# Edge sums of a graph network: from a TensorE product in step 0 to u8 rows, VectorE and ScalarE in step 1

## The chip, the cores and the metric

The kernel runs on one core of a Trainium2 chip. The metric is the device time of one execution in microseconds (us). A core has five engines with a queue each: TensorE (PE, with weight loads as PEld), VectorE (DVE), ScalarE (ACT), GpSimd (POOL) and SyncE (SP, which here only starts transfers). ScalarE and GpSimd start transfers from their queues too.

## The reference

Four graph layers over 4096 nodes with 256 features; `adj` is a 4096 x 4096 float32 matrix of zeros and ones. Each layer is followed by a residual and a layer norm.

```python
# layer 0: deg = adj.sum(1); relu([x, adj @ x / max(deg, 1)] @ W + b)
# layer 1: R = (adj + I) / row sum; two steps n = 0, 1:
#   A  = top-p attention of Xa: softmax(q k^T), keep the largest until their sum is 0.9
#   Xf = R @ Xf ; Xa = A @ Xa ; Z += Xf @ U1[n].T + Xa @ U2[n].T
# layer 2 (the change concerns its edge term):
neighbor_node_features = adj @ node_features
neighbor_edge_features = jnp.einsum('ij,ji->i', adj, edge_features)[:, None]   # edge_features = adj
support = jnp.concatenate((node_features, neighbor_node_features, neighbor_edge_features), axis=1)
out = support @ weight + bias
# layer 3: relu((d^-1/2 (adj + I) d^-1/2 @ x) @ W + b)
```

The edge term is one number per node: the sum over j of adj[i,j] * adj[j,i].

## The kernel before

Nodes go in 32 tiles of 128 (NT = 32). A row of 4096 columns is worked in NLC = 8 pieces of LC = 512 columns, which is GP = 4 blocks of 128. Layer 0 loads the adjacency blocks with transfers from GpSimd that cast float32 to u8, multiplies, and leaves a u8 copy in DRAM (`adj8_d`). Layers 1 to 3 read that copy with SP.

Layer 1 is `run_step(n)` for n = 0, 1. Its loop over i from -2 to 31 is pipelined: while tile i is applied, the logits of tile i+2 are made, and the selection of tile i+1 runs on VectorE. `pieces` walks the eight pieces g of an iteration. For each it emits: the logits of the next tile (L385, copied out by ScalarE at L386); in step 0 the sparse product with gathered rows (L734; gathers on GpSimd at L643), in step 1 four transposes (L717), their copy `at` on ScalarE (L720) and the product with `xa` (L742); then `neighbours`, one piece of an R product (adjacency loaded by SP at L652, cast by ScalarE at L654, multiplied at L657); then the operations that `run_step` has put at piece g. The latter hold the largest values (L404), exponentials (L423 in step 0, L427 in step 1), the search for the threshold, `settle` with passes over the row (L629, L634) and the layer norm, whose power is taken on GpSimd (L194). Rows whose threshold needs more care are put off and worked as jobs between the tiles; a conditional block on VectorE stands in each job.

In step 0 `neighbours` also makes the edge sums: `adjn`, the blocks of the other orientation, is loaded by GpSimd with a cast to u8 (L663), cast by ScalarE (L666), and multiplied with the same weights as R (L669) into the bank `nef_ps`. The diagonal of the 128 x 128 result is taken on VectorE at L683 and written to a column of `nef`. Layer 2 reads `nef` at L1110. Because `nef_ps` takes the bank "nef", R products of step 0 all use the bank "acc".

The order on each engine is fixed when the program is built: a scheduler takes the instructions in the order of the program text, lets ready ones pass those that wait, and works with estimated durations. `issue_after(x)` puts instructions on x's engine behind x. A pool's tile with `bufs=k` has k buffers, and a writer waits until the readers of k tiles ago are done.

Of the kernel before, what the change touches and what calls it, by code (L numbers as in the profile page):

```python
# [45 lines left out]


@with_exitstack
def gnn_stack(ctx, tc, x, adjt, adjn, w0, b0, w1, w2t, w3t, u1t, u2t, ln_g, ln_b, w2, b2, w3, b3, out):

# [59 lines left out]
    list_d = [dram.tile([N + P, 1], I32, name=f"list{n}_d") for n in range(STEPS)]  # L112

    adj8_d = [dram.tile([P, NT, P], U8, name=f"adj8_{it}_d") for it in range(NT)]
    h_d = dram.tile([N + P, D], F32, name="h_d")
    k_d = dram.tile([N + P, P], F32, name="k_d")

# [207 lines left out]

    with tc.tile_pool(name="l1", bufs=1, reuse_waits="tile") as l1:

        cur = {"late": False, "n": 0, "nef_done": False}


        FIRST = [[range(k * NT // 16, (k + 1) * NT // 16) for k in range(2)]]
# [313 lines left out]

        GP = LC // P

        def neighbours(n, i, g, acc_r, pn, xf):

            if g % 2 == 0:  # L650
                cur["a8"] = cur["w"].tile([P, 2 * GP, P], U8, tag="adj8", name="adj8", bufs=3)
                nc.sync.dma_start(cur["a8"], adj8_d[i][:, g * GP : (g + 2) * GP, :])  # L652
            a = cur["w"].tile([P, GP, P], F32R, tag="adjq", name="adjq", bufs=2)
            nc.scalar.copy(a, cur["a8"][:, g % 2 * GP : (g % 2 + 1) * GP, :])  # L654
            for j in range(GP):
                jt = g * GP + j
                nc.tensor.matmul(acc_r, a[:, j, :], xf[:, jt, :], start=(jt == 0), stop=False)  # L657
            if g + 1 == NLC:
                nc.tensor.matmul(acc_r, ident_r, xf[:, i, :], start=False, stop=True)
            if pn is not None:  # L660
                if g % (NLC // 2) == 0:
                    cur["b8"] = cur["w"].tile([P, NT // 2, P], U8, tag="adjn8", name="adjn8", bufs=2)
                    nc.gpsimd.dma_start(cur["b8"], adjn[i, :, g * GP : g * GP + NT // 2, :])  # L663
                b = cur["w"].tile([P, GP, P], F32R, tag="adjn", name="adjn", bufs=2)
                k = g % (NLC // 2) * GP
                nc.scalar.copy(b, cur["b8"][:, k : k + GP, :])  # L666
                for j in range(GP):
                    jt = g * GP + j
                    nc.tensor.matmul(pn[:, :P], a[:, j, :], b[:, j, :], start=(jt == 0),  # L669
                                     stop=(jt == NT - 1))  # L670

        def r_acc(i):

            return ps_acc.tile([P, 512], F32, tag=("acc", "nef")[i % 2 if cur["nef_done"] else 0], name="acc_r", bufs=1)

        def r_end(i, acc_r, pn):
            xf_new = work.tile([P, D], F32, tag="xf_new", name="xf_new", bufs=1)
            nc.scalar.activation(xf_new, acc_r[:, :D], AF.Copy, scale=rs[:, i : i + 1])
            nc.vector.scalar_tensor_tensor(xf_new, acc_r[:, D:], rs[:, i : i + 1], xf_new, op0=ALU.mult, op1=ALU.add)
            if pn is not None:  # L680

                junk = spare_row.bitcast(F32)[:, :P]
                nc.vector.scalar_tensor_tensor(junk, pn[:, :P], 1.0, ident, op0=ALU.mult, op1=ALU.mult,  # L683
                                               accum_out=nef[:, i : i + 1])
            nc.sync.dma_start(rows(xf_d, i), xf_new)

        def r_product(n, i, xf):

            acc_r, pn = r_acc(i), None
            if n == 0:  # L690
                pn = ps_acc.tile([P, 512], F32, tag="nef", name="nef_ps", bufs=1)
            for g in range(NLC):
                neighbours(n, i, g, acc_r, pn, xf)
            r_end(i, acc_r, pn)

        def pieces(n, st, nxt, ops, rs_now=()):


            G = GP
            few = st is not None and sparse(st)  # L700
            if st is not None:
                e = st["e"]
                acc_a = half("acc")
                if "xf" not in st:
                    fetch(n, st)
            with_r = st is not None and len(rs_now) > 0
            if with_r:
                i, = rs_now
                acc_r, pn = r_acc(i), None
                if n == 0:  # L710
                    pn = ps_acc.tile([P, 512], F32, tag="nef", name="nef_ps", bufs=1)
            ats = {}

            def turn(g):
                ps = ps_tr.tile([P, 4, P], F32, tag="tr", name="at_ps")
                for j in range(G):
                    nc.tensor.transpose(ps[:, j, :], e[:, (g * G + j) * P : (g * G + j + 1) * P], ident)  # L717
                at = cur["w"].tile([P, G, P], F32, tag="at", name="at", bufs=2)
                ats[g] = at
                nc.scalar.copy(at[:, :G, :], ps[:, :G, :])  # L720

            if st is not None and not few:
                turn(0)
            for g in range(NLC):
                if nxt is not None:
                    logits_chunk(nxt["e"], nxt["q"], g)
                if few:
                    per = KEPT // NLC
                    for k in range(g * per, (g + 1) * per):
                        if k % 4 == 0:  # L730
                            dg = cur["w"].tile([P, 4, P], F32, tag="at", name="dg", bufs=2)
                            nc.vector.tensor_mul(dg, ident[:, None, :].to_broadcast([P, 4, P]),
                                                 st["w"][:, k : k + 4, None].to_broadcast([P, 4, P]))
                        nc.tensor.matmul(acc_a, dg[:, k % 4, :], st["G"][k], start=(k == 0), stop=(k == KEPT - 1))  # L734
                        if k + 8 < KEPT:
                            gather(st, k + 8)
                elif st is not None:
                    if g + 1 < NLC:
                        turn(g + 1)
                    for j in range(G):  # L740
                        jt = g * G + j
                        nc.tensor.matmul(acc_a, ats[g][:, j, :], cur["xa"][:, jt, :], start=(jt == 0),  # L742
                                         stop=(jt == NT - 1))
                if with_r:
                    neighbours(n, i, g, acc_r, pn, cur["xf"])
                for f in ops.get(g, ()):
                    f()
            if st is None:
                for i in rs_now:
                    r_product(n, i, cur["xf"])  # L750
            else:
                xa_new = work.tile([P, D], F32, tag="xa_new", name="xa_new", bufs=1)
                nc.scalar.activation(xa_new, acc_a, AF.Copy, scale=st["sc"])
                if n + 1 < STEPS:
                    put(xa_d, st, xa_new)
                st["xa"] = xa_new
            if with_r:
                r_end(i, acc_r, pn)

        def put(dst, st, t):  # L760

# [27 lines left out]
        def mix(n, st):  # L789

            xt = transposed(st["xf"], st["xa"])
            ps = half("mm")
            for c in range(4):
                u = cur["u1" if c < 2 else "u2"]
                nc.tensor.matmul(ps, xt[:, c, :], u[:, c % 2, :], start=(c == 0), stop=(c == 3))  # L795
            h = work.tile([P, D], F32, tag="h", name="h")
            nc.vector.tensor_add(h, ps, st["res"])
            if n + 1 < STEPS:
                put(h_d, st, h)

                ps = half("mm")
                for c in range(2):
                    nc.tensor.matmul(ps[:, :P], xt[:, 2 + c, :], w3t_sb[:, c, :], start=(c == 0), stop=(c == 1))
                up = upper(ps[:, :P])
                kt = work.tile([P, P], F32, tag="kt", name="kt", bufs=1)
                nc.scalar.copy(kt[:, :DA], up[:, :DA])
                nc.vector.tensor_sub(kt[:, DA:], ps[:, DA:P], up[:, DA:])
                put(k_d, st, kt)
            return h
# [107 lines left out]
        def run_step(n, es):  # L917
# [37 lines left out]
            for i in range(-2, NT):  # L955
# [21 lines left out]
                if 0 < i + 2 < NT - 1:  # L977
                    turned = []
                    g = 1 if n else 6
                    at(g - 1, lambda i, turned: turned.append(transposed(cur["xa"][:, i + 3, :])), i, turned)  # L980
                    at(g, lambda turned: cur["qs"].append(query(None, turned[0])), turned)
                if cd is not None:
                    peak_groups(cd)
                    at(1, exp_rows, cd)
# [32 lines left out]
            if n == 0:  # L1017
# [4 lines left out]
                cur["late"] = True  # L1022
                fetch(n, jobs[0]["st"])
                cur["late"] = False
                cur["nef_done"] = True
                for i in range(FIRST[1][0][0]):
                    r_product(1, i, cur["next"])
            todo = []
            if n > 0:

                z_room(es[1 - NT % 2])
# [167 lines left out]
```

## Time and profile before

| | us |
|---|---|
| median of 3 runs (lowest to highest) | 3316.28 (3312.99 to 3319.80) |
| the profiled execution | 3319.24 |
| its span, first to last instruction | 3317.5 |

The mean granted TensorE clock is 0.967 of full speed. Busy shares of the span: TensorE 91%, VectorE 72%, ScalarE 57%, GpSimd 24%. These are means over stages that differ. The writes of `xa_new` (L753) mark the tiles: in step 0 from 476.5 to 1337.6, in step 1 from 1526.7 to about 2561; layers 2 and 3 fill the time from 2785 to the end. A row of the page's groups gives line, engine, operation, output and input tiles, count, then busy time, mean duration in ns, and the engine's idle time just before with what ended it.

### The profile page before, as it was taken

Reading aid. Unit: us, or ns where it says so; the run is one execution under the profiler, and the core shown is the slowest. Engines: PE = TensorE matmul, PEld = TensorE weight load, DVE = VectorE, ACT = ScalarE, POOL = GpSimd, SP = SyncE. Lnnn points to the kernel's source line nnn. Section 1 sums busy time; section 2 is a strip of 40 time slices with the busy share of each in tenths; the row PEclk is TensorE's granted clock in tenths of the full one; section 3 lists DMA queues with packets and bytes.
Section 4 is the critical chain, followed back from the end, with each engine's and each line's share of the span. In section 5 each row is a group of like instructions: output and inputs, shape, how many; then the busy total and the mean of one; then the engine's idle time right before and its main releaser. Section 6 shows DMA issues by size and latency. Waiting matters only on the chain. (4 is left out here: it accounts for less than half of the span.)

```text
span 3317.5 us, 46380 instructions
## 1 busy us (share of the span) xinstructions
PE 3005.6 (91%) x14600; PEld 2455.0 (74%) x14600; DVE 2392.3 (72%) x7113; ACT 1883.1 (57%) x3170; POOL 782.1 (24%) x916
## 2 busy tenths in 40 slices
PE   4999878999999997789989898989999786999998
PEld 4888767888888885567877777777788544888886
DVE  5888858878777776357988897888799673444444
ACT  4555566777777774455545454555455333666664
POOL 1111146666666665100000001000100001000000
PEclk9999989999999998889999999999999898999999
DMA  8888367777777776241000211011011133333332
GB/s 161 140 140 139 72 104 126 139 138 139 138 132 140 138 135 140 63 131 32 24 23 25 33 36 32 25 32 39 25 37 30 42 131 125 110 108 107 102 108 81
DMA packets 247906, 300.30 MB, mean 91 GB/s; under 512 B 34688, under 2 KB 201536, under 8 KB 247648
## 3 DMA queue, kind: packets, MB, share of 16 engines
q0 software_dynamic: 46624, 105.07, 22.7%
q1 hardware_dynamic: 184576, 176.73, 18.6%
q10 hardware_dynamic: 16448, 15.42, 1.5%
q8 instruction: 118, 1.93, 0.3%
q14 instruction: 140, 1.15, 0.1%
HBM read 331.17 MB, written 66.58 MB: 120 GB/s over the span
## 5 line engine op out<-in xcount | busy, mean ns | idle before, releaser
L657 PE MATMUL acc_r<-xh,adjq 128*128 128x512 f32 x2048 | 615.1, 431 | 25.3 <-ACT adjq L654 13.4
L742 PE MATMUL acc_bank<-xa,at 128*128 128x256 f32 x2304 | 569.6, 388 | 33.0 <-ACT at L720 32.5
L643 POOL DMA_INDIRECT G<-x_d,cols x512 | 499.4, 975 | 300.7 <-PE acc_bank L734 161.9
L742 PEld LDWEIGHTS acc_bank<-xa,at 128*128 128x128 f32 x2304 | 425.2, 194 | 94.8 <-ACT at L720 43.3
L654 ACT CAST adjq<-adj 128x512 fp32r<-128x512 uint8 x512 | 316.0, 619 | 294.5 <-PE acc_r L657 94.5
L657 PEld LDWEIGHTS acc_r<-xh,adjq 128*128 128x128 f32 x2048 | 380.4, 192 | 120.0 <-ACT adjq L654 43.5
L404 DVE MAX8 cand<-e 128x8 f32<-128x256 f32 x1024 | 381.9, 416 | 93.0 <-ACT e L386 92.0
L194 POOL TENSOR_TENSOR rstd<-ve,mhalf 128x1 f32<-128x1 f32 x168 | 102.3, 609 | 1374.4 <-DVE ve L192 1336.7
L386 ACT COPY e<-lg 128x512 f32<-128x512 f32 x552 | 319.0, 584 | 177.4 <-PE lg L385 176.4
L385 PE MATMUL lg<-kS,q 128*128 128x512 f32 x1104 | 393.5, 442 | 9.9 <-ACT e L386 9.6
L1093 ACT CAST a<-a 128x1024 fp32r<-128x1024 uint8 x256 | 268.0, 1048 | 147.5 <-PE acc L1096 119.3
L734 PE MATMUL acc_bank<-G,dg 128*128 128x256 f32 x1024 | 276.6, 390 | 51.5 <-DMA G<-x_d,cols 40.4
L501 DVE FIND_INDEX8 cols<-top,e 128x8 uint32<-128x4096 f32 x64 | 282.8, 4419 | 0.0
L1096 PE MATMUL acc<-xh,a 128*128 128x512 f32 x1024 | 254.9, 402 | 16.9 <-ACT a L1093 13.2
L170 PE MATMUL acc<-xh,a 128*128 128x512 f32 x1024 | 257.9, 404 | 13.3 <-ACT a L253 13.3
L734 PEld LDWEIGHTS acc_bank<-G,dg 128*128 128x128 f32 x1024 | 194.0, 193 | 101.1 <-DMA G<-x_d,cols 48.9
L720 ACT COPY at<-at_ps 128x512 f32<-128x512 f32 x296 | 173.6, 588 | 114.0 <-PE at_ps L717 90.1
L1096 PEld LDWEIGHTS acc<-xh,a 128*128 128x128 f32 x1024 | 190.5, 189 | 60.3 <-ACT a L1093 15.2
L1096 PE MATMUL acc<-yh,a 128*128 128x512 f32 x1024 | 233.7, 390 | 0.0
L170 PEld LDWEIGHTS acc<-xh,a 128*128 128x128 f32 x1024 | 191.7, 190 | 55.1 <-ACT a L253 13.5
L1096 PEld LDWEIGHTS acc<-yh,a 128*128 128x128 f32 x1024 | 192.1, 188 | 39.8
L253 ACT CAST a<-a 128x1024 fp32r<-128x1024 uint8 x128 | 133.9, 1048 | 129.6 <-PE acc L170 117.4
(282 smaller groups left out, 5001.5 us busy)
## 6 DMA issues: line engine op xcount, KB each, us to landing
adj<-adj_d SPq DMA_DIRECT2D x256, 128.0 KB, 2.7
a<-adj_d SPq DMA_DIRECT2D x256, 128.0 KB, 2.3
a<-in_adjt POOLq DMA_DIRECT2D x64, 256.0 KB
adj_d<-a SPq DMA_DIRECT2D x64, 256.0 KB, 3.7
adjn<-in_adjn POOLq DMA_DIRECT2D x64, 256.0 KB
x_d<-x SPq DMA_DIRECT2D x65, 128.0 KB, 1.8
G<-x_d,cols POOLq DMA_INDIRECT x512
xf_d<-xf_new SPq DMA_DIRECT2D x64, 128.0 KB, 4.9
```

Source lines behind the costliest of these rows:

```text
L170: nc.tensor.matmul(acc, a[:, j, :], halves(jt), start=(jt == 0), stop=(jt == NT - 1))
L385: nc.tensor.matmul(pl[:, :LC], q[k], kS[:, s], start=(k == 0), stop=(k == 1))
L386: nc.scalar.copy(l[:, s], pl[:, :LC])
L404: nc.vector.max(dst[:, 8 * g : 8 * g + 8], src[:, g * GW : (g + 1) * GW])
L501: nc.vector.max_index(st["at"][:, 8 * r : 8 * r + 8], t8, st["e"][:, :N])
L643: nc.gpsimd.indirect_dma_start(out=g, out_offset=None, in_=x1_d, in_offset=bass.IndirectOffsetOnAxis(ap=st["at"][:, k : k + 1], axis=0))
L654: nc.scalar.copy(a, cur["a8"][:, g % 2 * GP : (g % 2 + 1) * GP, :])
L657: nc.tensor.matmul(acc_r, a[:, j, :], xf[:, jt, :], start=(jt == 0), stop=False)
L734: nc.tensor.matmul(acc_a, dg[:, k % 4, :], st["G"][k], start=(k == 0), stop=(k == KEPT - 1))
L742: nc.tensor.matmul(acc_a, ats[g][:, j, :], cur["xa"][:, jt, :], start=(jt == 0), stop=(jt == NT - 1))
L1093: nc.scalar.copy(a, a8)
L1096: nc.tensor.matmul(acc, a[:, j, :], halves(jt), start=(jt == 0), stop=(jt == NT - 1))
```

## The change

The product of step 0 goes: `adjn` is no longer an input, and with it go L663, L666, L669 and L683. Instead `adj` and its transpose come in as plain rows (`adjr`, `adjc`). In step 1 each piece g of iteration i starts one transfer on GpSimd for tile i+2 (`edge_cast`), DRAM to DRAM, which casts 128 x 1024 float32 (512 KB) to u8 (128 KB): even g for `adjr`, odd g for `adjc`, eight per tile, 256 in all.

For the tile that is being applied, `edge_sums` runs once per piece in three stages. Two loads on ScalarE's queue bring 128 x 512 bytes of both (`r8`, `c8`, two buffers each). One piece later VectorE takes their bitwise AND, read as 128 x 128 int32, into `r8`. Another piece later ScalarE copies `r8` to `c8` with an accumulated sum into a column of `ns`; after the eighth piece VectorE adds the eight columns into `nef`. Loads and sums are put behind the latest `at` copy of ScalarE. What is left after the last tile is finished there.

Further: `adj8` is loaded per piece (64 KB, 512 loads) instead of per two pieces (128 KB, 256 loads), with three buffers as before; R products alternate between the banks "acc" and "nef" in step 0 too; `kt` moves to the pool of the step.

```diff
...
+    adjr8_d, adjc8_d = ([dram.tile([P, N], U8, name=f"{k}_{it}_d") for it in range(NT)] for k in ("adjr8", "adjc8"))
...
-        def neighbours(n, i, g, acc_r, pn, xf):
-
-            if g % 2 == 0:
-                cur["a8"] = cur["w"].tile([P, 2 * GP, P], U8, tag="adj8", name="adj8", bufs=3)
-                nc.sync.dma_start(cur["a8"], adj8_d[i][:, g * GP : (g + 2) * GP, :])
+        def neighbours(i, g, acc_r, xf):
+
+            a8 = cur["w"].tile([P, GP, P], U8, tag="adj8", name="adj8", bufs=3)
+            nc.sync.dma_start(a8, adj8_d[i][:, g * GP : (g + 1) * GP, :])
...
-            if pn is not None:
-                if g % (NLC // 2) == 0:
-                    cur["b8"] = cur["w"].tile([P, NT // 2, P], U8, tag="adjn8", name="adjn8", bufs=2)
-                    nc.gpsimd.dma_start(cur["b8"], adjn[i, :, g * GP : g * GP + NT // 2, :])
-                b = cur["w"].tile([P, GP, P], F32R, tag="adjn", name="adjn", bufs=2)
-                k = g % (NLC // 2) * GP
-                nc.scalar.copy(b, cur["b8"][:, k : k + GP, :])
-                for j in range(GP):
-                    jt = g * GP + j
-                    nc.tensor.matmul(pn[:, :P], a[:, j, :], b[:, j, :], start=(jt == 0),
-                                     stop=(jt == NT - 1))
...
-            return ps_acc.tile([P, 512], F32, tag=("acc", "nef")[i % 2 if cur["nef_done"] else 0], name="acc_r", bufs=1)
+            return ps_acc.tile([P, 512], F32, tag=("acc", "nef")[i % 2], name="acc_r", bufs=1)
+
+        def edge_cast(i, g):
+
+            src, dst = ((adjr, adjr8_d), (adjc, adjc8_d))[g % 2]
+            s = slice(g // 2 * 2 * LC, (g // 2 + 1) * 2 * LC)
+            nc.gpsimd.dma_start(dst[i][:, s], rows(src, i)[:, s])
+
+        edges = []
+
+        def edge_sum():
+
+            i, g, ns, r8, c8 = edges.pop(0)
+            nc.scalar.activation(c8, r8, AF.Copy, accum_out=ns[:, g : g + 1])
+            if g + 1 == NLC:
+                nc.vector.tensor_reduce(nef[:, i : i + 1], ns, axis=AX.X, op=ALU.add)
+
+        def edge_product():
+            i, g, ns, r8, c8 = edges[-1]
+            nc.vector.tensor_tensor(r8.bitcast(I32), r8.bitcast(I32), c8.bitcast(I32), op=ALU.bitwise_and)
+
+        def edge_sums(i, g, at):
+
+
+            if g == 0:
+                cur["ns"] = small("ns", NLC)
+            with tc.issue_after(at.ins):
+                if len(edges) > 1:
+                    edge_sum()
+                s = slice(g * LC, (g + 1) * LC)
+                r8, c8 = (cur["w"].tile([P, LC], U8, tag=k, name=k, bufs=2) for k in ("r8", "c8"))
+                nc.scalar.dma_start(r8, adjr8_d[i][:, s])
+                nc.scalar.dma_start(c8, adjc8_d[i][:, s])
+            if edges:
+                edge_product()
+            edges.append((i, g, cur["ns"], r8, c8))
...
-                nc.vector.scalar_tensor_tensor(junk, pn[:, :P], 1.0, ident, op0=ALU.mult, op1=ALU.mult,
-                                               accum_out=nef[:, i : i + 1])
...
-                nc.scalar.copy(at[:, :G, :], ps[:, :G, :])
+                turns["at"] = nc.scalar.copy(at[:, :G, :], ps[:, :G, :])
...
+                if n > 0 and st is not None and st["tile"] is not None:
+                    edge_sums(st["tile"], g, turns["at"])
                 if with_r:
-                    neighbours(n, i, g, acc_r, pn, cur["xf"])
+                    neighbours(i, g, acc_r, cur["xf"])
...
-                kt = work.tile([P, P], F32, tag="kt", name="kt", bufs=1)
+                kt = cur["w"].tile([P, P], F32, tag="kt", name="kt", bufs=1)
...
+                if n > 0 and i + 2 < NT:
+                    for g in range(NLC):
+                        at(g, edge_cast, i + 2, g)
...
+            if edges:
+                edge_product()
+                while edges:
+                    edge_sum()
...
-        "adjn": blocks.transpose(2, 1, 0, 3),
+        "adjr": adj,
+        "adjc": adj.T,
...
```

## The prediction

> **What bounds the kernel now.** I read the slices first, then the windows by stage, then the timeline of one tile. The change leaves layer 0 (to 387 us) and layers 2 and 3 (from 2785 us) alone, so its worth is read from step 0 (387 to about 1346) and step 1 (about 1440 to 2700). Columns of the windows: stretch, length, busy time of TensorE, its weight loads, VectorE, ScalarE, GpSimd, granted clock, DMA share, GB/s.
>
> ```profile
> core 0: us, PE busy (x) PEld busy (x) DVE busy (x) ACT busy (x) POOL busy (x), PEclk, DMA share, GB/s
> 591.00:864.00 273.00, 259.99 (x1389) 221.86 (x1388) 218.98 (x639) 196.47 (x389) 177.59 (x190) 1.00 0.77 138
> 1527.00:1697.00 170.00, 162.36 (x856) 136.22 (x855) 154.16 (x530) 90.26 (x152) 13.56 (x18) 1.00 0.09 24
> 2118.00:2183.00 65.00, 63.15 (x324) 52.68 (x324) 63.40 (x231) 36.46 (x62) 3.35 (x5) 1.00 0.11 33
> ```
>
> The first row is ten tiles of step 0 at 27.3 us each (distance between two writes of xa_new, L753). TensorE is busy 95%, VectorE 80%, ScalarE 72%: step 0 hangs on TensorE. The second is six tiles of step 1 at 28.3 us: TensorE 96%, VectorE 91%, ScalarE 53%. The third lies where step 1 also works off the put-off rows: TensorE and VectorE both 97%. Step 1 is nearly full on two engines, and ScalarE, GpSimd and the DMA engines (0.09 to 0.11) have room.
>
> What the change removes, in the groups of instructions (line, engine, operation, tiles, count, busy us, mean ns, idle before):
>
> ```profile
> L666 ACT CAST adjn<-adjn 128x512 fp32r<-128x512 uint8 x256 | 159.2, 622 | 1.9 <-DMA adjn<-in_adjn 1.9
> L669 PEld LDWEIGHTS nef_ps<-adjn,adjq 128*128 128x128 f32 x1024 | 156.9, 192 | 23.9 <-ACT adjn L666 0.7
> L669 PE MATMUL nef_ps<-adjn,adjq 128*128 128x128 f32 x1024 | 149.4, 265 | 0.0
> ```
>
> The 149.4 us overlap with neighbours, so I take the cost from starts in TensorE's timeline of one piece (start, duration):
>
> ```profile
> 913.24 1.27 PE L657 MATMUL acc_r<-xh,adjq 128*128 128x512 f32 x4
> 914.35 0.56 PE L669 MATMUL nef_ps<-adjn,adjq 128*128 128x128 f32 x4
> 914.74 0.41 PE L180 MATMUL tr<-ident,x 128*128 128x128 f32 x2
> ```
>
> From 914.35 to 914.74, four of these matmuls hold TensorE 0.39 us.
>
> **What the Trainium skill says.** "DMA: Bandwidth & Descriptors", section "SWDGE vs HWDGE vs iDMA": a transfer that casts must be issued from GpSimd. The trace agrees: both casting loads (L250, L663) are on GpSimd's queue, so the new casts come there too. The same page, "Issuing engines are not separate DMA queues": queues of all engines run on the same 16 DMA engines. The trace agrees in kind: 128 KB loads land in 2.3 us in layers 2 and 3, in 2.7 us where step 0's casts run.
>
> **The change, part by part.**
>
> Step 0, TensorE. Per tile 8 pieces x 0.39 = 3.1 us go; 27.3 becomes 24.2 if nothing else holds the tile. VectorE's timeline from 865.0 to 892.3 has 4.7 us of gaps, so 22.6 us are occupied; without the trace sum (L683, 0.28 + 0.08) 22.2. GpSimd: 16 gathers at 0.95 + 0.30 between two, and one list write of 1.3, 21.3 us. ScalarE loses 8 casts that occupy about 0.52 each and has room. So TensorE stays the bound, but with three engines above 21 of 24 us I expect more waits than today's 1.2 us a tile: 24.5 us, a gain of 2.8. Some 29 tiles run in this state (477 to 1279): 29 x 2.8 = 81 us. Tiles 0 to 3 of R lie at the start (387 to 477), where ScalarE is busy 79%: 3.1 us each less, some 10 after what ScalarE keeps. **Step 0: -91 us.** Bounds: -112 (3.1 for all 32 tiles, half of the 1.2 us of waits too, the start without loss: 99 + 13), and -45 (VectorE or GpSimd holds the tile at 25.9).
>
> Step 0, the rest. The 64 casting loads of adjn (1 MB of source each) leave the DMA engines and 64 issues of 0.59 leave GpSimd: only relief. The adj8 loads become twice as many of half the size: 256 more issues of 0.32 us on SP over both steps, under 15% of a tile's time on SP; three buffers of four blocks hold three pieces, and a piece takes 3 us against a landing of 2.7, so I cost it at nothing. If that cover went (R alone takes 1.0 us a piece in the tail of step 0, five tiles), three pieces cover 2.9 us and a wait of 0.2 a piece is an estimate: 40 x 0.2 = 8 us at most. The second accumulator bank in step 0 frees the start of an R tile: nothing, at most 0.5 us a tile.
>
> Step 1, VectorE. Per tile 8 products, 128x128 as int32, and one reduction of 8 columns. The nearest row is 128x128 of L265 at 292 ns; the skill's "VectorE: DVE Perf Modes", section "The TRN2 errata — SBUF-src ops pay a fixed extra latency per instruction", gives (N+151)/0.96 for two tensors of 32 bits, which for 128 is an estimate of 291: agreement. Back to back, starts are 0.2 us apart (L204 at 878.92, next at 879.12), so 8 x 0.21 + 0.15 = 1.8 us a tile, 58 us over 32 tiles. VectorE's gaps from 1527 to 2561 add up to about 120 us, TensorE's to 66, but they are uneven: in 2118 to 2183 VectorE has 1.6 us for two tiles. Bounds: nothing (all in gaps) and 58 and a half more (waits that its lateness makes). I take 40.
>
> Step 1, ScalarE. Per piece one sum, 128x512 of u8 with an accumulator. Nearest rows: casts of that size at 619 ns, and 189 for the accumulator read (L423). "ScalarE: Activation LUTs", section "What ACT_TABLE_LOAD costs", gives 186 + 0.833 N, 613 for 512, and 93 ns of overlap: the trace's 619 and 0.52 between starts agree. So 0.71 us, and two load issues of 0.33 (L290 on ScalarE's queue, 334 ns), partly under the activation before: 0.35 counted. 8 x 1.06 = 8.5 us a tile; the gaps of ScalarE are 79 us in 170, 13.2 us a tile. It fits, and rises to about 83%. What is queued behind it matters more: the copies at (L720) and e (L386), for which TensorE waits. Bounds: nothing, and 2 x 0.7 us a tile = 45. I take 12.
>
> Step 1, casts. 256 transfers on GpSimd at 0.59 (L663): 4.7 us a tile, GpSimd is at 8%. A rstd (L194) that meets one is late by up to 0.6, twice a tile, a third of the time: 0.4 us of VectorE in a tile, half of it hidden: 6 us. The DMA engines: layer 0 takes 0.86 x 10.5 = 9.0 us of them per tile for 2 MB of source and 0.9 MB of plain traffic; at layers 2 and 3's 0.40 for 125 GB/s the plain part is 2.9, so 3 us per MB of source. Step 1 gets 4 MB a tile: 12 us, a share of about 0.5. Casts wait for nothing, so some may leave early in a bunch (L663 is issued at 849.63 and first used near 864); beside the loads at 1346 to 1440 they would cost up to 15, I take 5. The loads r8 and c8 get one piece of 3.5 us before the product, against 2 to 2.7 to land: covered; without cover see the first rival.
>
> After the last tile two sums and a reduction: under 2 us. **Step 1: 40 + 12 + 6 + 5 + 2 = +65.** Layers 2 and 3: 0.
>
> **Sum.** -91 + 65 = -26 beside the profiled execution, whose time is 3319.2 (span 3317.5), 3 above the median of 3316.3. On the median: 3290. Part of each step-1 item would hide under another (one late piece covers the next), which I put at 6: 3284.
>
> **Rivals.**
> First, slower: **ScalarE waits in order.** A sum waits for VectorE's product, a product for its loads; VectorE has single instructions of 4.4 us (L629, L469), and behind the waiting sum stand at and e, hence TensorE. For: ScalarE's 3.71 us exponential already makes TensorE wait 1.08 us for at at 1587.86. Against: three stages leave a piece or more to each hand-over. It decides from 2.8 us a tile (91 / 32); at 0.5 us a piece, 4 us a tile, it costs 128 instead of 65: 3316 - 91 + 128 = 3353.
> Second, **the gaps take it all:** with 120 us of gaps on VectorE, step 1 costs only about 15: 3316 - 91 + 15 = 3240. For: TensorE gets no new work there. Against: the 97% window.
> Third, **step 0 doesn't follow:** VectorE and the gathers hold the tile near 25.9, -45, and step 1 costs 55: 3326. For: 22.2 and 21.3 of 24; against: the waits on G in 700 to 850 are only 6 us.
> That the change doesn't do what it says is no rival of weight: L669 and L666 go by the diff.
>
> **How the numbers follow.** Forecast (3255 to 3306) 0.46, gaps take it 0.24, ScalarE waits 0.21, step 0 doesn't follow 0.09. A measurement of this kernel can tell about 0.2%, 6.6 us. The second case and nine tenths of the forecast are faster; of the third and fourth most are slower. So 0.66 faster, 0.09 same, 0.25 slower. The range leaves out the best of the second case (a fifth of it, 0.05) and the upper part of the first rival (under half, 0.09), with room for the bounds of the steps: 3208 to 3358.
>
> **What would show it.** Tiles of step 0 near 24.5 us and no L669; step 1 tiles without R near 29.5 to 30 instead of 28.3; VectorE at 95% or more there; DMA share about 0.5. Wrong if step 0 stays above 26, or if ScalarE's sums show waits on VectorE and TensorE's wait for at grows by more than 3 us a tile.

## The result and the profile after

The change makes the kernel slower: 3552.81 us (median of 4 runs, 3544.53 to 3556.42) against 3314.64 us for the kernel before on the same chip, a ratio of 1.070 (95% interval 1.0688 to 1.0714). I had forecast 3284, with 3208 to 3358 as the range. On another chip the ratio was 1.072 (1.0706 to 1.0742). Each group of experiments below ran on one chip beside the kernel before, which took 3315 to 3325 us on some chips and 3353 to 3363 on others; so ratios are taken within a group.

The first view is the page of slices of the changed kernel (span 3553.4 us, so 88.8 us a slice): busy tenths of TensorE, its granted clock, the share of the DMA engines.

```profile
PE   1555579889999999689988988999989687999998
PEclk9766689999999999789999999999999798999999
DMA  9999998255666666542211112122222133433332
```

In the first five slices, up to 444 us, TensorE is busy about half or less and the DMA engines are full. Later, where step 1 runs (slices 20 to 32), the DMA share is only 0.1 to 0.2. I had expected about 0.5 there. The windows by stage say the same; columns are stretch, length, busy time of TensorE, weight loads, VectorE, ScalarE, GpSimd, then clock, DMA share, GB/s. First the kernel before in layer 0, then the kernel after in layer 0, step 0 and the first tiles of step 1.

```profile
core 0: us, PE busy (x) PEld busy (x) DVE busy (x) ACT busy (x) POOL busy (x), PEclk, DMA share, GB/s
5.00:387.00 382.00, 339.55 (x1664) 283.92 (x1664) 302.76 (x755) 189.10 (x268) 56.26 (x97) 1.00 0.80 135
...
60.00:360.00 300.00, 300.00 (x1486) 252.19 (x1484) 257.03 (x660) 160.74 (x227) 45.90 (x83) 1.00 0.86 137
```

```profile
60.00:360.00 300.00, 160.70 (x574) 121.88 (x574) 95.77 (x231) 64.08 (x86) 104.05 (x198) 0.72 1.11 129
...
760.00:1427.00 667.00, 632.82 (x2977) 522.10 (x2976) 600.06 (x1771) 436.02 (x862) 463.43 (x477) 0.98 0.64 135
1674.00:1890.00 216.00, 191.67 (x961) 156.69 (x962) 182.04 (x658) 136.87 (x276) 20.76 (x21) 0.96 0.20 53
```

A DMA share above 1.00 stands so in the view; I read it as full. In the same 300 us TensorE issues 574 matmuls instead of 1486. The timeline of GpSimd shows why: all 256 casts (L668) are issued between 4.5 and 459.6 us. First the two groups of the casts (busy us, mean ns, then the idle time just before them and what ended it), then two waits of 60 to 460 us, both in the kernel after:

```profile
L668 POOL DMA_DIRECT2D adjr_d<-in_adjr x128 | 66.9, 523 | 125.3 <-DMA adjc_d<-in_adjc 61.5 <-DMA adjr_d<-in_adjr 33.6 <-DMA a<-in_adjt 25.9
L668 POOL DMA_DIRECT2D adjc_d<-in_adjc x128 | 66.6, 520 | 125.2 <-DMA adjr_d<-in_adjr 59.2 <-DMA adjc_d<-in_adjc 33.2 <-DMA a<-in_adjt 31.3
```

```profile
engine line waited for: us in total, times, longest us
ACT agg L286 <- DVE rdeg L278: 262.0, 12, 33.7
DVE x L201 <- POOL rstd L196: 249.8, 12, 35.8
```

GpSimd issues a cast in 0.52 us and stands ahead of the casts for 250 us in all, nearly always until an earlier transfer has landed. Behind the casts stand layer 0's own loads of the adjacency (L252) and its rstd (L196), up to 35.8 us each time; VectorE waits for rstd, ScalarE for VectorE, TensorE for both.

The writes of `xa_new` cut the whole span into stages (us):

| stage | before | after | difference |
|---|---|---|---|
| start to the first xa_new | 476.5 | 732.4 | +255.9 |
| step 0, first to last xa_new of its loop | 818.2 | 715.6 | -102.6 |
| from there to the first of step 1 | 232.0 | 226.3 | -5.7 |
| step 1, to the last write | 1237.8 | 1316.2 | +78.4 |
| the rest, mostly layers 2 and 3 | 553.0 | 562.9 | +9.9 |

They sum to +235.9, the difference of the spans. The first row is a net figure: the change also takes the loads and the product of adjn away from the last part of this stretch, as e11_held_again shows below. The +9.9 of the last row was not traced; of the kernels here, e1 to e15 with them, those that do products and sums in step 1 have 557 to 563 us there, the others 546 to 553.

The waits of the changed kernel in step 1 (1674 to 2860 us), where the new instructions run:

```profile
engine line waited for: us in total, times, longest us
...
ACT c L675 <- DVE r L681: 108.1, 79, 8.3
DVE r L681 <- DMA c<-adjc_d: 88.5, 37, 7.8
```

The product (L681) waits for its loads in 37 pieces, and the sum (L675) for the product in 79, though the casts were long done.

### The profile page after: what moved, and what is told of

Its sections match the earlier page's. It is cut to its first block, busy times and chain, and to the rows that moved or that the text cites. A ratio compares the mean times of both kernels' runs of the same rounds, so it can differ in the third digit from the quotient of the medians.

```text
span 3553.4 us, 46237 instructions
## 1 busy us (share of the span) xinstructions
PE 2990.4 (84%) x13576; PEld 2389.1 (67%) x13576; DVE 2420.8 (68%) x7337; ACT 1910.5 (54%) x3426; POOL 877.8 (25%) x1108
## 5 line engine op out<-in xcount | busy, mean ns | idle before, releaser
L658 PE MATMUL acc_r<-xh,adjq 128*128 128x512 f32 x2048 | 632.6, 435 | 51.0 <-ACT adjq L655 48.3
L196 POOL TENSOR_TENSOR rstd<-ve,mhalf 128x1 f32<-128x1 f32 x168 | 101.2, 602 | 1370.8 <-DVE ve L194 1345.9
L1115 ACT CAST a<-a 128x1024 fp32r<-128x1024 uint8 x256 | 268.1, 1049 | 156.9 <-PE acc L1118 125.3
L172 PE MATMUL acc<-xh,a 128*128 128x512 f32 x1024 | 271.1, 420 | 34.3 <-ACT a L255 34.3
L1118 PE MATMUL acc<-xh,a 128*128 128x512 f32 x1024 | 261.8, 410 | 17.6 <-ACT a L1115 14.5
L172 PEld LDWEIGHTS acc<-xh,a 128*128 128x128 f32 x1024 | 201.5, 200 | 77.5 <-ACT a L255 35.0
L387 PEld LDWEIGHTS lg<-kS,q 128*128 128x128 f32 x1104 | 196.4, 194 | 66.8 <-ACT e L388 39.9
L1118 PE MATMUL acc<-yh,a 128*128 128x512 f32 x1024 | 237.7, 393 | 0.0
L1118 PEld LDWEIGHTS acc<-xh,a 128*128 128x128 f32 x1024 | 194.0, 192 | 63.8 <-ACT a L1115 16.2
L675 ACT ACTIVATE c<-r 128x512 uint8<-128x512 uint8 x256 | 162.4, 634 | 118.9 <-DVE r L681 112.3
## 6 DMA issues: line engine op xcount, KB each, us to landing
a<-in_adjt POOLq DMA_DIRECT2D x64, 256.0 KB
adj_d<-a SPq DMA_DIRECT2D x64, 256.0 KB
```

Of the source, the lines that this page charges most:

```text
L172: nc.tensor.matmul(acc, a[:, j, :], halves(jt), start=(jt == 0), stop=(jt == NT - 1))
L387: nc.tensor.matmul(pl[:, :LC], q[k], kS[:, s], start=(k == 0), stop=(k == 1))
L1115: nc.scalar.copy(a, a8)
L1118: nc.tensor.matmul(acc, a[:, j, :], halves(jt), start=(jt == 0), stop=(jt == NT - 1))
```

## The experiments

**Do the casts alone cost layer 0 its 256 us?** `e2_before_casts` adds them, unread, to the kernel before; `e15_half_casts` adds only those of adjr.

```diff
...
+                if n > 0 and i + 2 < NT:
+                    for g in range(NLC):                 # e15: range(0, NLC, 2)
+                        at(g, edge_cast, i + 2, g)
```

> The kernel before, with the 256 casts added as the change has them and nobody reading their rows. Theory A: they leave in layer 0 here too, step 0 begins some 255 us later, and the time is about 3315 + 255 = 3570 with steps 0 and 1 at their old tile times (27.3 and 28.3 us). Theory B: the delay is spread over steps 0 and 1, layer 0 grows by less than 100. If the loss came from the waits of the edge sums in step 1 (theory C), this kernel is within 60 of before.

Measured: 3618.58 against 3362.58, +256.0 us, ratio 1.076 (1.0737 to 1.0786). The window of layer 0 is that of the changed kernel within 2%:

```profile
60.00:360.00 300.00, 163.11 (x574) 123.14 (x574) 95.80 (x231) 64.19 (x86) 104.08 (x199) 0.72 1.11 129
```

Its step-1 tiles are 28.2 us as in the kernel before. So the casts alone make the loss in layer 0, and no product or sum is needed for it.

> The kernel before with 128 casts instead of 256 (those of adjr), unread and free to leave in layer 0. If layer 0 pays by bytes, as DMA engines that are full: half of 256, 115 to 140 us above before (ratio 1.034 to 1.042). If the first half fills what was free in layer 0: under 80 (1.024). If it is the queue's length that counts: near 256.

Measured: 3477.93 against 3355.02, +122.9 us, ratio 1.037 (1.0353 to 1.0387): half the casts, half the time.

```profile
60.00:360.00 300.00, 210.80 (x913) 169.11 (x914) 165.24 (x410) 105.05 (x144) 81.66 (x153) 0.83 1.04 137
```

Layer 0 pays in proportion. e15 halves the number of casts and their bytes alike, so it doesn't tell the two apart; nor does a run separate full DMA engines from GpSimd's own queue, where layer 0's loads stand behind the casts. A rough sum fits the bytes. 256 casts read 134 MB. The Trainium skill, "DMA: Bandwidth & Descriptors", section "Measured (HBM→SBUF, 128 partitions, SWDGE, issued from GpSimd)", has 16 MB in 79.0 us, 425 GB/s; at that rate 134 MB are an estimate of 316 us of all DMA engines, and the kernel before leaves 0.20 of 382 us free in layer 0, 76 us. 316 - 76 = 240; the runs show 256. No run here measured that rate, and these casts end in DRAM and not in SBUF. The prediction's own 3 us per MB gives 384 - 76 = 308. So the agreement is one of size only.

**Held in step 1, are they hidden?** In `e1_held` (and again, on a chip where before is faster, `e11_held_again`) a cast follows the latest rstd or list write on GpSimd, which in step 1 belongs to the tiles there.

```diff
...
-        nc.gpsimd.tensor_tensor(r, ve, mhalf, op=ALU.pow)
+        turns["pool"] = nc.gpsimd.tensor_tensor(r, ve, mhalf, op=ALU.pow)
...
-            nc.gpsimd.dma_start(dst[i][:, s], rows(src, i)[:, s])
+            with tc.issue_after(turns["pool"].ins):
+                nc.gpsimd.dma_start(dst[i][:, s], rows(src, i)[:, s])
```

> The changed kernel with each cast put behind the latest instruction of GpSimd's queue in the text (a power of the layer norm or a list write of step 1), so that it leaves about two tiles ahead of its use. Theory A (place): the loss is that the casts, which wait for nothing, leave in layer 0 and hold up its loads for 255 us; held back, layer 0 is as before (step 0 begins near 387 us), and the time is 3553 - 255 = 3298, up to 3330 if the casts slow step 1 beside them. Theory B (work): the casts take their DMA time from somebody wherever they run, so step 1 loses most of the 255: above 3450.

> The changed kernel with the casts held in step 1 as in e1_held. If the place of the casts is most of the loss and step 1 can carry them half hidden, as the unread held casts did (+71 and +99): 3380 to 3420 where before is 3320 (ratio 1.02 to 1.03). Rival (the products' loads are late behind the casts, and that chain is the larger part): 3480 or more (ratio over 1.05).

> The changed kernel as it is, beside the next ones on one chip. First xa_new near 730 us, time 6 to 8% over before.

Measured: e1_held 3651.09, ratio 1.086 (1.0835 to 1.0879). e11_held_again 3531.97, 1.062 (1.060 to 1.0635), with the changed kernel itself at 3565.45 and 1.072 on that chip. Layer 0 is whole again, and the loss has moved: step 1 takes 1541 us in e11 instead of 1238. My theory that the place is most of the loss fell; e1 and e11 lie where its rivals had them. The casts of e11 leave from 1186 us on, the first of them at the end of step 0. The first xa_new is at 456.0 in e11 and at 734.3 in e10_after_again on the same chip, so by this pair the casts cost the start 278 us. The kernel before has it at 476.5 on a chip of like speed: the removal of adjn gives some 20 us there, and +255.9 in the table beside the +256.0 of e2 is in part chance. The waits of e11_held_again in step 1:

```profile
DVE r L682 <- DMA c<-adjc_d: 314.1, 68, 15.6
ACT c L676 <- DVE r L682: 202.6, 97, 10.2
```

ScalarE loses time in one more way, which these waits don't hold. The issue of a load of r8 or c8 on its queue takes 0.33 to 0.45 us as a rule, but beside held casts up to 6.4: in e11 23 of them take over 1 us, 73 us together, against 7 and 11 us without casts (e12 below).

**What of that is casts, what loads, what work?** These kernels differ from others by one part: `e3_no_edges` (no casts, loads, products, sums), `e4_no_casts` and `e12_no_casts_again` (both loads read the adjacency copy, so the sums are of other data), `e8_no_loads` (neither casts nor loads; products and sums on two fixed pairs of buffers), `e9_held_no_loads` (the same with held casts), and `e7_before_held` (the kernel before with held, unread casts).

```diff
...
 # e3: without the calls of edge_sums and edge_cast
-                    edge_sums(st["tile"], g, turns["at"])
-                        at(g, edge_cast, i + 2, g)
 # e4, e12: without the call of edge_cast, and
-                nc.scalar.dma_start(r8, adjr8_d[i][:, s])
-                nc.scalar.dma_start(c8, adjc8_d[i][:, s])
+                nc.scalar.dma_start(r8.rearrange("p (j i) -> p j i", i=P), adj8_d[i][:, g * GP : (g + 1) * GP, :])
+                nc.scalar.dma_start(c8.rearrange("p (j i) -> p j i", i=P), adj8_d[i][:, g * GP : (g + 1) * GP, :])
 # e8, e9
-                nc.scalar.dma_start(r8, adjr8_d[i][:, s])
-                nc.scalar.dma_start(c8, adjc8_d[i][:, s])
+                r8, c8 = still[g % 2]
...
```

> The changed kernel without edge sums: no casts, loads, products or sums, nef is set to zero. It prices the removal alone. By the traces (step 0 shorter by 102, the rest as before) 3315 - 102 = 3213; by the recorded sum (-91) 3224. If the halved adjacency loads or the new bank order cost something in steps 0 or 1, it is above 3230.

> The changed kernel without casts: both loads of each piece read the u8 copy that layer 0 leaves anyway, so the sums are other numbers; loads, products and sums are all there. Theory A: layer 0 as before, step 1 as in the changed kernel (+78), so 3553 - 255 = 3298. Against the kernel without edge sums it prices loads, product and sum: about 80 us by the traces, 59 by the recorded working (40 + 12 + 2 and a few). If casts and edge sums hurt each other in step 1 (theory B), this one is well below the one with held casts.

> The changed kernel without casts, both loads reading the adjacency copy, on a chip of the faster sort. Work alone cost 3217 there, held casts with the work 3316, held casts with loads and work 3532. If loads are late on their own (one piece of cover is too little even without casts): 3300 or more (ratio over 0.99). If they are late only behind casts: within 40 us of 3217 (0.968 to 0.98).

> The changed kernel without casts and without the loads of r8 and c8: products, sums and reductions run on two fixed pairs of buffers. It shows the price of the work on VectorE and ScalarE alone. My prediction had 40 + 12 for it, less for hiding: 30 to 50 us over the kernel without edge sums (ratio to before 1.000 to 1.005). Rival (the lateness of the loads makes most of the 57 us that loads, products and sums cost together): 0 to 20 us over it (0.990 to 0.996).

> As the last one, with the 256 casts held in step 1, unread. If the chain of late r8, product, sum, at carries the cost of held casts: within 60 us of the one without casts (ratio to before under 1.02). If the casts hold up others by themselves (adj8 loads, rstd on GpSimd's queue): 150 to 270 us above it (1.045 to 1.085).

> The kernel before with the 256 casts added and held in step 1, nobody reads them. If transfers that nobody waits for still cost step 1 (rstd behind casts on GpSimd, adj8 loads late): some 100 to 250 us above before (ratio 1.03 to 1.075). Rival (what hurts in step 1 is only that products wait for r8 and c8, and sums for products): within 30 us of before (ratio under 1.01).

Measured:

| kernel | us | ratio to before (95%) | step 1, us |
|---|---|---|---|
| e3_no_edges | 3326.64 | 0.990 (0.9871 to 0.9923) | 1256 |
| e4_no_casts | 3383.68 | 1.006 (1.0042 to 1.0085) | 1301 |
| e12_no_casts_again | 3356.63 | 1.001 (0.9989 to 1.0028) | 1285 |
| e8_no_loads | 3217.36 | 0.968 (0.9661 to 0.9704) | 1255 |
| e9_held_no_loads | 3316.52 | 0.998 (0.9967 to 0.9991) | 1328 |
| e7_before_held | 3395.79 | 1.021 (1.0193 to 1.0227) | 1291 |

The lower three ran on one chip, beside before at 3324.46; e11 ran on another, beside before at 3324.78. e3, e4 and e12 ran on chips where before is slower, so the totals that I had forecast for them, from times on faster chips, don't apply. Step 1 can be compared: it differs little with the chip (1238 us in the kernel before, 1228 in e2_before_casts and in e15_half_casts on slower chips; 1541 in e11, 1533 in e1).

Read by step 1, the parts are these. Without any edge work and with whole adjacency loads it takes 1232 us (e5 below), with halved loads and still no edge work 1256 (e3): halving costs about 24 (28 against e2 on e3's own chip). Products and sums on top of that, without loads, give 1255 (e8): their work costs nothing that shows, where I had forecast 30 to 50 us for it. The loads of r8 and c8 add 30 (e12), 46 (e4) and 61 (the changed kernel, 1316). Held casts add 99 us to the whole (e9 less e8), and without edge work 71 (e7); both lie between the two cases that I had forecast. The loads of r8 and c8 beside held casts add 215 more (e11 less e9). So loads and casts together are far worse than their sum. Where nobody waits for r8, what is late behind the casts is the adjacency of R; in e9_held_no_loads in step 1:

```profile
ACT adjq L655 <- DMA adj<-adj_d: 105.0, 28, 10.1
PEld acc_r L658 <- ACT adjq L655: 78.4, 45, 10.0
```

In e8_no_loads the first of these is 38.4 us. The skill's section "Issuing engines are not separate DMA queues", which the prediction had cited, says that the transfers of all engines' queues interleave on the same 16 DMA engines. The trace agrees: beside casts that GpSimd issues, the waits for SP's loads rise from 38.4 to 105.0 us.

**Why are the loads so late beside casts?** The timeline of GpSimd in e11_held_again, one tile of step 1:

```profile
1621.42 0.54 POOL L196 TENSOR_TENSOR rstd<-ve,mhalf 128x1 f32<-128x1 f32 x1 [2.17 <-DVE ve L194]
1621.92 0.61 POOL L669 DMA_DIRECT2D adjr_d<-in_adjr  x1
1622.52 0.53 POOL L669 DMA_DIRECT2D adjc_d<-in_adjc  x1
1623.04 0.52 POOL L669 DMA_DIRECT2D adjr_d<-in_adjr  x1
1633.22 2.02 POOL L579 DMA_INDIRECT list_d<-ids,slots  x1 [9.66 <-DVE r L682]
1635.25 0.59 POOL L669 DMA_DIRECT2D adjc_d<-in_adjc  x1
1635.84 0.53 POOL L669 DMA_DIRECT2D adjr_d<-in_adjr  x1
...
1637.37 0.52 POOL L669 DMA_DIRECT2D adjc_d<-in_adjc  x1
```

The eight casts of a tile leave in two bunches, three behind rstd and five behind the list write; the five are 2.5 MB of source, issued in 2.6 us. They leave together because the list write itself has waited 9.66 us for VectorE. `e14_paced` puts a one-column copy ahead of each cast that reads that piece of the new logits; `e13_held_early` leaves the bunches and loads two pieces ahead instead of one.

```diff
...
 # e14
+            with tc.issue_after(nc.gpsimd.tensor_copy(pace, e[:, g * LC : g * LC + 1]).ins):
 # e13
+            if len(edges) >= 2:
+                edge_product(2)
...
-                r8, c8 = (cur["w"].tile([P, LC], U8, tag=k, name=k, bufs=2) for k in ("r8", "c8"))
+                r8, c8 = (cur["w"].tile([P, LC], U8, tag="r8", name="r8", bufs=3), w3t_sb[:, g % 2, :].bitcast(U8))
...
```

> As e11_held_again, but each cast follows a one-column copy on GpSimd that reads its own piece of the new logits, so that casts leave one by one, and not four and more in a row behind a rstd. If the bunches make the loads late: 100 us or more less, under 3430 (ratio under 1.033). If one cast ahead of a load is enough to make it late: within 50 us of 3532 (1.047 to 1.077).

> As e11_held_again, but r8 and c8 are loaded two pieces ahead of the product instead of one (three buffers of r8, the sum in place, c8 in the space of a weight that step 1 no longer reads). If late loads carry most of the 216 us that the loads cost beside casts: a third to two thirds of it goes, 3390 to 3460 (ratio 1.02 to 1.042). Rival (the loads cost by their traffic or their issues on ScalarE, not by being late): over 3500 (ratio over 1.053).

Measured on one chip, before at 3355.02: e14_paced 3485.18, ratio 1.040 (1.0378 to 1.0413); e13_held_early 3607.30, 1.077 (1.0740 to 1.0794). e1_held, on a chip with before at 3362.58, had 1.086. Across these two chips, spreading the casts takes back about half of what held casts with loads lost, and one piece more of cover a tenth. e14 lies between its two forecasts (under 1.033, and 1.047 to 1.077): bunches are part of the lateness, not all. e13 missed its forecast and lies where its rival had it (over 1.053), that the loads cost by their traffic or their issues and not by being late. The rival alone doesn't carry the 215: e12 has the same traffic and issues of loads, without casts, at 1285 us in step 1. But e13 doesn't refute it for loads beside casts, and the long issues on ScalarE speak for a share of it. The other reading is that waits at the product reached 15.6 us in e11, and one more piece of 3.5 us hides little of such a wait; no run separates the two. In e14's timeline the casts leave one by one:

```profile
1612.68 0.18 POOL L668 COPY slots<-e 128x1 f32<-128x1 f32 x1 [0.59 <-ACT e L388]
1613.11 0.52 POOL L669 DMA_DIRECT2D adjr_d<-in_adjr  x1 [0.24 <-issue]
1615.39 0.18 POOL L668 COPY slots<-e 128x1 f32<-128x1 f32 x1 [1.76 <-ACT e L388]
1615.82 0.52 POOL L669 DMA_DIRECT2D adjc_d<-in_adjc  x1 [0.25 <-issue]
```

and the waits of step 1 fall, but do not go:

```profile
DVE r L683 <- DMA c<-adjc_d: 184.4, 59, 10.0
...
ACT c L677 <- DVE r L683: 116.6, 79, 6.8
```

Step 1 takes 1395 us there, against 1285 without casts (e12). The 110 us between them I put down to loads late behind single casts; that is argued from these waits, not shown by a run of its own.

**What do the halved adjacency loads cost?** `e5_e3_wide` is e3_no_edges with the loads of the kernel before.

```diff
...
-            a8 = cur["w"].tile([P, GP, P], U8, tag="adj8", name="adj8", bufs=3)
-            nc.sync.dma_start(a8, adj8_d[i][:, g * GP : (g + 1) * GP, :])
+            if g % 2 == 0:
+                cur["a8"] = cur["w"].tile([P, 2 * GP, P], U8, tag="adj8", name="adj8", bufs=3)
+                nc.sync.dma_start(cur["a8"], adj8_d[i][:, g * GP : (g + 2) * GP, :])
...
```

> The kernel without edge sums, but with the adjacency of R loaded as before, 128 KB for two pieces. Theory (the halved loads ate step 0's gain: three buffers of one piece do not cover landings of 6 us): step-0 tiles near 24.5 us, ScalarE's waits for adj8 in step 0 back to those of the kernel before, time 80 to 100 us below before's (ratio 0.970 to 0.976). Rival (VectorE and the gathers hold the tile, as my third rival had it): no better than 50 below before, tiles near 26.

Measured: 3160.99, ratio 0.950 (0.9478 to 0.9517), 163 us below before, where I had forecast 80 to 100. Most of the difference to e3 is the chip and not the loads: e8_no_loads, beside it on the same chip and with halved loads, has step-0 tiles of 24 us too. From the first to the last xa_new of step 0, e5 takes 692.3 us and e8 719.0, so halving costs 27 us there, beside the 24 in step 1. With whole loads a settled tile of step 0 takes 22.4 us, and TensorE doesn't wait any more:

```profile
886.00:1120.00 234.00, 233.63 (x1117) 192.72 (x1116) 222.54 (x633) 164.67 (x329) 172.39 (x178) 1.00 0.68 144
```

On the chips where the kernel before is slower, step 0 keeps 27 to 28 us a tile without the edge product, with halved loads (e3) and, below, with whole ones (y3).

**Is there a better place?** `y1_layer2` holds the casts in step 1, reads none of them there, has the whole adjacency loads, and makes the edge sums in layer 2, 1024 columns at a time: loads on SP, AND and every second sum on VectorE, the others on ScalarE. `y2_split` moves the casts of adjr to step 0. `y3_paced` is y1 with e14's spread casts. `y5_mult` is y3 with product and sum of VectorE's pieces in one instruction.

```diff
...
-                a = l23.tile([P, JP, P], F32R, tag="adjt", name="a", bufs=4)
+                a = l23.tile([P, JP, P], F32R, tag="adjt", name="a", bufs=3)
...
+                nc.vector.tensor_tensor(r8.bitcast(I32), r8.bitcast(I32), c8.bitcast(I32), op=ALU.bitwise_and)
+                if c % 2:
+                    nc.vector.tensor_scalar(c8, r8, 1.0, 0.0, op0=ALU.mult, op1=ALU.add, accum_out=ns[:, c : c + 1])
+                else:
+                    nc.scalar.activation(c8, r8, AF.Copy, accum_out=ns[:, c : c + 1])
...
+            edges_l2(it)
 # y5, for odd c instead of AND and sum
+                    nc.vector.scalar_tensor_tensor(c8, r8, 1.0, c8, op0=ALU.mult, op1=ALU.mult, accum_out=ns[:, c : c + 1])
...
```

> A version: casts held in step 1 with nobody reading them there, wide adjacency loads as before, and products and sums in layer 2, where VectorE is busy 45% and the DMA share is 0.36 (pieces of 1024 columns loaded on SP, AND and every second sum on VectorE, the others on ScalarE). Casts cost 70 to 100 in step 1, layer 2 0 to 40: 163 gained without edge sums leaves a ratio of 0.97 to 0.99. If layer 2 can't carry it (ScalarE's adjacency casts behind sums, loads late): over 1.0.

> As y1_layer2, but the casts of adjr run in step 0, where the kernel before had hidden as many bytes of casts for adjn, and only those of adjc in step 1. If the cost of casts in step 1 goes by bytes: 35 to 50 less there, and 0 to 30 more in step 0: ratio 0.955 to 0.985. If the gathers on GpSimd's queue wait behind casts: step-0 tiles above 25 us and no gain over y1_layer2.

> y1_layer2 with the casts of step 1 leaving one by one, each behind a one-column copy of its piece of the logits, as in e14. If bunches of casts are what the put-off rows' tiles and the adjacency loads wait for in y1_layer2 (74 us in step 1 and ahead of it): 30 to 60 us less, ratio 0.98 to 0.99. If the casts cost by their share of the DMA engines however they leave: as y1_layer2, 0.998 to 1.003.

> As y3_paced, and in layer 2 VectorE takes product and sum of its pieces in one instruction (multiply with an accumulator) instead of an AND and a sum: two instructions of 423 ns less a tile. Layer 2 of y1_layer2 took some 80 us more than without edge sums, with VectorE busy 72% and TensorE waiting for its agg. If VectorE's order is what holds layer 2: 10 to 35 us below y3_paced (ratio 0.97 to 0.985). If the loads beside layer 2's own are: no difference.

Measured: y1_layer2 3327.05, ratio 1.0006 (0.9997 to 1.0015), no different from before, where I had forecast 0.97 to 0.99. y2_split 3523.59, 1.059 (1.0570 to 1.0606). y3_paced 3417.58, 1.020 (1.0173 to 1.0216), and y5_mult 3401.58, 1.013 (1.0093 to 1.0159), both on a chip with before at 3353.28.

In y1, step 1 takes 1284 us (51 more than e5), the stretch ahead of it 23 more, and the time after it, mostly layers 2 and 3, 633 against 550. Its layer 2, and that of the kernel before:

```profile
2750.00:3030.00 280.00, 240.90 (x1021) 185.94 (x1020) 200.21 (x515) 199.17 (x312) 14.51 (x26) 0.98 0.60 183
```

```profile
2800.00:3050.00 250.00, 247.45 (x1098) 198.34 (x1099) 114.04 (x325) 163.01 (x232) 15.92 (x29) 1.00 0.38 117
```

VectorE and ScalarE rise to 71% each, and TensorE falls from 99 to 86%. But not all of the 83 us is edge work: from first to last of the matmuls, layer 2 takes 330 us against 278 in e5 (L1118 in y1), and layer 3, which has no edge work at all, 261 against 236. The one edit that reaches layer 3 is that these versions give `a` three buffers there instead of four; a version with four was not run. y5 wins 14 us over y3 after step 1 (618 against 632). y2 failed by its rival: the gathers of step 0 stand behind casts on GpSimd's queue, and tiles rise from 22.9 us in y1 to 29.4. With half as many casts in step 1, it takes 1284 us there like y1, where I had forecast 35 to 50 less: so here held casts don't cost step 1 by their bytes. Its waits from 500 to 1300 us:

```profile
PE acc_bank L750 <- DMA G<-x_d,cols: 137.8, 27, 9.8
...
POOL G L645 <- DMA adjr_d<-in_adjr: 62.7, 39, 3.7
```

y3 missed both of its forecasts in the total, but answers the open question on the casts without readers: its step 1 takes 1233.5 us, against 1232.5 in e5 without casts, at a DMA share of 0.56. Spread out, and with nobody waiting for them, 256 casts cost step 1 nothing that shows. That y3's ratio is above y1's comes from step 0, which on that chip has tiles of 28 us. No version that I ran with the edge sums in it beats the kernel before. y5 on a chip of the other sort might: y1's 3327 less about 50 in step 1 and 14 in layer 2 is an estimate of 3263. It was not run there.

## Why the prediction was wrong, step by step

- **The step that failed is "Step 1, casts".** It placed the casts by the program text, in step 1, and gave "some may leave early" 5 us, 15 at most. All 256 left early. The scheduler lets a ready instruction pass those that wait, and a cast that reads an input and writes a buffer of its own is ready at 4 us. e2 prices it at 256 us, e15 shows half of that for half of the casts. The numbers to see it were in the text itself: 3 us per MB and 4 MB a tile are 384 us for 32 tiles, and layer 0 had 0.14 to 0.20 of its 387 us free. I compared the bunch with one transfer that I saw leave some 14 us ahead of its use, not with all 256.
- **The halved adjacency loads, "I cost it at nothing", 8 us at most:** they cost 27 in step 0 (e5 against e8) and about 24 in step 1 (e3 against e5). The number under it, a landing of 2.7 us "where step 0's casts run", is the median over the whole run: between 500 and 1240 us the kernel before shows 6.6 us as the median for these loads.
- **The loads r8 and c8, "covered":** wrong as well, with the same number. I set 3.5 us of cover against landings of 2 to 2.7 us. With the casts long over, these loads cost step 1 30 to 61 us (e12, e4 and the changed kernel against e8). Beside held casts they cost 215.
- **VectorE 40 and ScalarE 12 in step 1:** too high: products and sums cost nothing that shows (e8 against e3). The duration of one product was right: 282 ns measured beside my estimate of 291. VectorE did not reach 95%; it is at 84% in the first tiles, and it waits for loads. Tiles without R are 31.0 us on average, not 29.5 to 30. That step 1 as a whole came out at +78 where I had +65 is luck: about 24 from halved loads and the rest from late loads, where I had work.
- **rstd behind casts on GpSimd, 6 us:** the mechanism was real and at the wrong place. It held layer 0, at up to 35.8 us a time.
- **Step 0, -91:** near in number, by luck. Its tile fell to 23.8 us where I had 24.5, and its loop by 103; with some 20 at the start the gain is above my bound of 112. The product was worth more than I had: in e5 a settled tile falls from 27.3 to 22.4, 4.9 us where I took 2.8 and 3.1 at most. By the distances between the starts of TensorE's matmuls in the kernel before (591 to 838 us), the product held TensorE 3.8 us a tile; the rest is about the 1.3 us a tile in which TensorE had no work there, and which is gone in e5, where I had expected more waits. The halved loads then took a part back. On a chip where the kernel before is slower this step does not hold: e3 saves only 36 us in all, so there the third rival, that step 0 doesn't follow, came true.
- **The rivals:** the first, ScalarE waiting in order for products, did show (108 us of waits at L675) and is contained in the 78. None of the rivals held the case that the transfers run elsewhere, so the range left it out. The rival that ends slower should have been this one: its mechanism, its place and its price were all at hand.

## What to carry to other kernels

A transfer runs where its dependencies let it, not where the program text stands; before pricing one, ask what holds it, and if nothing does, price it where it can first run. Here 3 us per MB less the free share of layer 0 would have given some 308 us, an estimate from the kernel before alone, against the 256 to 278 measured. A stage's mean DMA share says little about a load's landing: transfers queued behind one waiting instruction leave as a bunch, and in e11, at a mean share of 0.53, products then waited up to 15.6 us for their loads. A change that comes with the main one, like the halved loads, needs a price of its own. Take the cover that a load needs from landings in its own stage beside its new neighbours.

## What the runs showed of the hardware that was not expected

- 256 casts of 512 KB from DRAM to DRAM cost a stage with full DMA engines 1.0 us each. Spread over step 1 they raise the DMA share from 0.14 (e5, 1690 to 2500 us) to 0.56 (y3's step 1, 1234 us), 0.42 x 1234 / 256 = 2.0 us of all 16 engines each, and the time by nothing. Why a cast keeps the engines busy for longer there than it costs in layer 0 was not tried.
- Beside held casts the issue of a 64 KB load on ScalarE's queue, else 0.33 to 0.45 us, took up to 6.4 us (e11), and ScalarE stood meanwhile.
- The same step-0 program (e4 and e8 differ only in step 1) has tiles of 27 us on one chip and 24 on another. In e3 on the first, four matmuls of 128x512 take 1.91 us in one tile and 1.28 in another, and the mean granted clock from 700 to 1100 us is 0.95:

```profile
745.14 1.91 PE L659 MATMUL acc_r<-xh,adjq 128*128 128x512 f32 x4
...
833.54 1.28 PE L659 MATMUL acc_r<-xh,adjq 128*128 128x512 f32 x4
```

  In layer 0 of the changed kernel, where TensorE mostly waits, the clock is 0.72; in e5 from 886 to 1120 us, where it never waits, 1.00. Pauses of TensorE and a lower clock go together in these windows; which comes first, and why only some chips show it in step 0, was not settled.
